# Degree sums by quarters of tokens and a block transpose on VectorE, with pairwise prices for TensorE's changes of use in the planner

## The chip, the cores and the metric

The kernel runs on one core of one Trainium2 chip. The metric is the device time of one execution in microseconds. A core has five engines that work side by side: TensorE (PE, matmuls and transposes; its weight loads are shown as PEld), VectorE (DVE), ScalarE (ACT), GpSimd (POOL) and SyncE (SP, which here only issues transfers). Each works through its own list of instructions in order and waits on semaphores for the others.

## What is computed

There are 64 independent graphs of 256 nodes with 256 features each, in float32, with an adjacency matrix of 256x256 for each. Four layers follow one another, and each is wrapped in `x = layernorm(x + layer(x))`. The change concerns the first layer:

```python
X = heads(lrelu(node_feats @ W_lin + b_lin))      # 4 heads of 64 features
q = heads(lrelu(node_feats @ W_q))
k = heads(lrelu(node_feats @ W_k))
att = sigmoid(einsum('bhxd,bhyd->bhxy', q, k) * scale)
adj_h = adj[:, None] * att
deg = sum(adj_h, axis=-1)                         # one number per head and node
dis = where(deg > 0, deg ** -0.5, 0)
A = dis[..., :, None] * adj_h * dis[..., None, :]
Y = einsum('bhxy,bhyd->bhxd', A, X)               # then a layernorm
```

Layer 1 is a masked softmax attention with 8 heads of 32 features, layer 2 a neighbour sum with an MLP of width 1024, layer 3 a graph attention with one head.

## The kernel before

**Layout.** A node index of 256 is two blocks of 128 partitions (`NB = 2`), and a tile of kind "s" holds 2 x 256 columns. For layer 0 the products `adj_h` are kept transposed: the partition is the node that is summed over, the columns are (head, block, node). `att` is that tile, 128 x 2048.

**The degrees (lines 441 to 465).** L445 adds the two blocks of summed nodes on DVE into two tiles `added`, each for two heads, with columns (head, node). L450 sums over the 128 partitions on PE: its weights are a 128x32 tile of ones, so that each head's sums for 256 nodes land, 32 times over, on a group of 32 partitions of `ps`. The four heads use the four groups of 32 columns of PE's array. Now the nodes lie along the columns, and they are wanted along the partitions. L453 copies the sums to SBUF on ACT (`deg`), L458 transposes the two 128x128 blocks on PE into another PSUM buffer (`pd`), and `D8` picks one of every 32 columns, which gives 8 numbers for each partition: for each block of nodes, four heads. L462 clamps them on DVE, L463 raises them to the power -0.5 on POOL, L464 puts 0 where the degree is 0 (`dis`), L468 scales the values `v` with it. L476 is the matmul with `att`, and after it `dis` scales the result.

**The planner.** The program is written as operations with an engine, an estimated cost in ns, the tiles read and written, and for PE a mode: "full", "rows" (the array split into groups of rows, L433 and L515), "columns" (split into groups of columns, L450, L476 and L551) or "transpose". `Plan.order` simulates the five engines with these costs and puts the operations of all graphs, which lie at different layers at the same time, in one order. Of all operations that are ready it always takes the one that can start first; among equals the one that is due first. An operation that needs a tile waits for a free buffer of its kind in this simulation; PSUM ("p") has 8. The resulting order is each engine's list of instructions. What counts here for PE is one line: an operation of another mode than the last one can start later by `CHANGE[mode]`, where `mode` is the one that is left.

```python
CHANGE = {"full": 0, "rows": 100, "columns": 140, "transpose": 60}
start = max(clock[op.engine] + (CHANGE[mode] if op.engine == "PE" and op.mode != mode else 0), op.ready)
```

So before, the same number served to choose and to advance PE's clock in the simulation. `SLOTS` gives the buffers of each kind, `PE_MM` the cost of a matmul over 256 columns (432 ns) and `PE_TR` that of a transpose (109 ns).

Of the kernel before, what the change touches and what calls it, by code (L numbers as in the profile page):

```python
# [11 lines left out]
OP = mybir.AluOpType  # L12

P = 128
NEG = -9000000000000000.0
TINY = 1.1754944e-38
# [3 lines left out]
PE_MM, PE_TR = 432, 109  # L20
AFTER = {"PE": 230, "DVE": 150, "ACT": 190, "POOL": 180, "SP": 3000}
ITSELF = {"PE": 0, "DVE": 95, "ACT": 110, "POOL": 60, "SP": 0}
CHANGE = {"full": 0, "rows": 100, "columns": 140, "transpose": 60}
TABLE_LOAD = 1430

DMA_KB, DMA_SEEN = 4, 1900

WORDS = {"s": 516, "d": 1024, "b": 2048, "c": 32, "p": 512, "h": 1024}
AHEAD = 12
NEAR = 1, 1, 3  # L30

ROUND = 0, 2, 5, 7
# [43 lines left out]
class Plan:  # L76
# [9 lines left out]
    def op(self, engine, cost, fn, w=(), r=(), turn=None, mode="full", after=None, size=0):  # L86
        pair = lambda x: x if isinstance(x, tuple) else (x, None)
        w, r = [pair(x) for x in w], [pair(x) for x in r]
        op = Op(engine, cost, fn, w, r, self.graph, turn, mode, after, size)
        op.table = turn is not None and engine == "ACT"  # L90
        if op.table:
            self.turns[turn] = self.turns.get(turn, 0) + 1
        self.ops.append(op)

    def order(self):
        for i, op in enumerate(self.ops):
            op.index = i
        for op in reversed(self.ops):
            op.due = min((nxt.due for nxt in op.after), default=4 * (min(op.graph + ROUND[3], self.graphs - 1 + TAIL[3]) + 1))
            if op.turn is not None:  # L100
                op.due = min(op.due, op.turn)
        clock = {e: 0.0 for e in AFTER}
        self.free = {k: [(0.0, i) for i in range(n)] for k, n in SLOTS.items()}
        turns, left = sorted(self.turns), dict(self.turns)
        turn, loaded, mode, moved = 0, None, "full", 0.0
        ready = {op for op in self.ops if not op.waits}
        done = []
        self.busy = {e: 0.0 for e in AFTER}
        while ready:
            best = None  # L110
            for op in ready:
                if (op.due - AHEAD if op.first else op.turn or 0) > turns[turn]:
                    continue
                start = max(clock[op.engine] + (CHANGE[mode] if op.engine == "PE" and op.mode != mode else 0), op.ready)
                need = {}
                for v in op.values:
                    if v.slot is None:
                        need[v.kind] = need.get(v.kind, 0) + 1
                for kind, n in need.items():
                    free = self.free[kind]  # L120
                    if len(free) < n:
                        break
                    start = max(start, sorted(free)[n - 1][0])
                else:
                    key = start, op.due, op.graph, op.index
                    if best is None or key < best[0]:
                        best = key, start, op
            if best is None:
                raise RuntimeError(f"the plan is stuck at {len(done)} of {len(self.ops)}")
            _, start, op = best  # L130
            op.start = start
            ready.discard(op)
            if op.table and op.turn != loaded:
                op.start, loaded = op.start + TABLE_LOAD, op.turn
            if op.engine == "PE":
                mode = op.mode
            end = clock[op.engine] = op.start + op.cost
            op.landed = end + op.seen
            if op.engine == "SP":
                moved = max(moved, end) + op.size * DMA_KB  # L140
                op.landed = max(op.landed, moved + DMA_SEEN)
            self.busy[op.engine] += op.cost
            done.append(op)
            op.takes = [v for v in op.values if v.slot is None]
            for v in op.takes:
                self.free[v.kind].sort()
                v.slot = self.free[v.kind].pop(0)[1]
            for v in op.values:
                v.uses -= 1
                v.end = max(v.end, op.landed)  # L150
                if not v.uses:
                    self.free[v.kind].append((v.end, v.slot))
            for nxt in op.after:
                nxt.waits -= 1
                nxt.ready = max(nxt.ready, end + ITSELF[op.engine] if nxt.engine == op.engine != "SP" else op.landed)
                if not nxt.waits:
                    ready.add(nxt)
            if op.table:
                left[op.turn] -= 1
                while turn < len(turns) - 1 and not left[turns[turn]]:  # L160
                    turn += 1
        assert len(done) == len(self.ops)
        self.span = max(op.start + op.cost for op in done)
        return sorted(done, key=lambda op: op.start)


def two(v):

    return v.t.rearrange("p (n c) -> p n c", n=2)
# [69 lines left out]
def graph(plan, nc, c, t, out, b):  # L239

    op = plan.op
    pe, dve, act, pool = nc and nc.tensor, nc and nc.vector, nc and nc.scalar, nc and nc.gpsimd
    NB = DB = 2
    N = D = 256
    H0, H1 = 4, 8
# [21 lines left out]
    def transposed(src):  # L267
        ps = Value("p", "ps", 2)
        transpose(lambda: two(ps), lambda: two(src), ps, src)
        return ps  # L270
# [27 lines left out]
    def copy(ps, name):  # L298
        dst = Value("s", name, 2)
        op("ACT", 466, lambda: act.copy(dst.t, ps.t), [dst], [ps])  # L300
        return dst
# [111 lines left out]
    for w, name in ((c.w0_q, "qT0"), (c.w0_k, "kT0")):  # L413
        ps = feature_major(w, xT)
# [4 lines left out]
    ps = token_major(xT, lambda: c.w0_l.t, [c.w0_l])  # L419
# [8 lines left out]
    def fn(pss=pss):  # L428
        for hp in range(H0 // 2):
            for m in range(NB):  # L430
                for i in range(2):
                    s = slice(i * HD0, (i + 1) * HD0)
                    pe.matmul(two(pss[2 * hp + i])[:, m, :], two(kT)[s, hp, m * P:(m + 1) * P], two(qT)[s, hp, :],  # L433
                              start=True, stop=True)
# [6 lines left out]
    ps = Value("p", "ps")  # L441
    added = [Value("s", "added") for _ in range(H0 // 2)]
# [3 lines left out]
           [added[i]], [(att, 2 * i), (att, 2 * i + 1)])  # L446

    def fn(ps=ps):
        for h in range(H0):
            pe.matmul(ps.t[h * 32:(h + 1) * 32, :N], c.ones, two(added[h // 2])[:, h % 2], start=True, stop=True)  # L450
    op("PE", PE_MM, fn, [ps], added, mode="columns")
    deg = Value("s", "deg")
    op("ACT", 258, lambda ps=ps: act.copy(deg.t[:, :N], ps.t[:, :N]), [deg], [ps])  # L453
    pd = Value("p", "ps")

    def fn():
        for n in range(NB):
            pe.transpose(pd.t[:, n * P:(n + 1) * P], deg.t[:, n * P:(n + 1) * P], c.ident)  # L458
    op("PE", 2 * PE_TR, fn, [pd], [deg], mode="transpose")
    dp, dis = Value("c", "dp"), Value("c", "dis")  # L460
    D8 = lambda: pd.t[:, :N].rearrange("p (g k) -> p g k", k=32)[:, :, 0]
    op("DVE", 50, lambda: dve.tensor_scalar(dp.t[:, :8], D8(), TINY, None, op0=OP.max), [dp], [pd])  # L462
    op("POOL", 1610, lambda: pool.tensor_tensor(dp.t[:, :8], dp.t[:, :8], c.mhalf, OP.pow), [dp], [dp])  # L463
    op("DVE", 83, lambda: dve.scalar_tensor_tensor(dis.t[:, :8], D8(), 0.0, dp.t[:, :8], op0=OP.is_gt, op1=OP.mult),  # L464
       [dis], [pd, dp])
    by_head = lambda ap: ap.rearrange("p (g d) -> p g d", d=HD0)
    dis_b = lambda: dis.t[:, :8, None].to_broadcast([P, NB * H0, HD0])
# [1 line left out]
    ps = Value("p", "ps", 2)  # L469
# [9 lines left out]
    y = Value("s", "y", 2)  # L479
    if b < NEAR[0]:  # L480
        ps = transposed(copy(ps, "yT"))
# [9 lines left out]
    mv, m = stats(y)  # L491
# [7 lines left out]
    ps = feature_major(c.w1_q, xT)  # L499
# [8 lines left out]
    for hq in range(H1 // 4):  # L508
# [9 lines left out]
        for pair in range(2):  # L518
            e = Value("d", "e", 4)
            for i in range(2):  # L520
                softmax(pss[2 * pair + i], negmask, HD1 ** -0.5, e,
                        lambda n, i=i, e=e: e.t[:, 256 * (2 * i + n):256 * (2 * i + n + 1)],
                        lambda n, i=i: 2 * i + n, r, lambda n, h=4 * hq + 2 * pair + i: 2 * h + n, turn(1, EXP))
            if b < NEAR[1]:
                eT = Value("d", "eT", 2)
                for i in range(2):
                    half = lambda v, i=i: v.t[:, 512 * i:512 * (i + 1)].rearrange("p (n c) -> p n c", n=2)
                    ps = Value("p", "ps", 2)
# [28 lines left out]
    ps = Value("p", "ps")  # L557
# [20 lines left out]
    ps = Value("p", "ps", 2)  # L578
# [10 lines left out]
    for j in range(0, HB, 2):  # L589
        ps = Value("p", "ps", 2)  # L590
# [17 lines left out]
    ps = Value("p", "ps")  # L608
# [21 lines left out]
    ps = Value("p", "ps", 2)  # L630
# [11 lines left out]

    xT3 = copy(transposed(x), "xT3") if b >= plan.graphs - NEAR[2] else far_transposed(x, "xT3")
    v3 = Value("s", "v3", 2)
    V3 = lambda: v3.full.rearrange("p (n c) -> p n c", n=2)
    s1 = lambda n: V3()[:, n, D:D + 1]
    for n in range(NB):
        ps = Value("p", "ps")
# [23 lines left out]
    ps = token_major(eT, lambda: V3()[:, :, :D], [v3])  # L672
    y3 = Value("s", "y", 2)
    mv, m = stats(ps, r3)
# [8 lines left out]
def gnn_stack_kernel(ctx: ExitStack, tc: tile.TileContext, t: dict, out: bass.AP):  # L683
# [36 lines left out]
    for b in range(B):  # L720
        plan.graph = b
        graph(plan, nc, c, t, out, b)
# [43 lines left out]
```

## Time and profile before

| | before |
|---|---|
| time, median of 3 runs | 2791.36 us (2789.9 to 2795.58) |
| span of the profiled execution | 2787.5 us |
| PE busy | 2739.8 us, 98% |
| DVE busy | 2483.4 us, 89% |
| ACT busy | 2138.6 us, 77% |
| POOL busy | 582.3 us, 21% |
| sums L450 on PE | 512 instructions, 40.2 us busy |
| copy L453 on ACT | 64 instructions, 23.9 us busy |
| transposes L458 on PE | 128 instructions, 24.7 us busy |

A row of the groups reads: line, engine, operation, output and inputs by their names in the program, output and input shapes, number of instructions; then busy time in us, mean duration in ns; then the idle time of the engine before these instructions and which instruction ended most of it. In a row of the timeline the first number is the start in us, the second how long the group of instructions lasted. Durations of matmuls overlap, so that for PE the starts tell more than the durations. In the view of waits a row gives who waited for whom, the sum in us, the number of waits and the longest.

### The profile page before, as it was taken

To read this page: it belongs to the slowest core of one execution; us is meant where nothing else is said; L and a number is where in the kernel's file an instruction comes from. 1 tells how busy PE (TensorE), PEld (TensorE's weight loads), DVE (VectorE), ACT (ScalarE), POOL (GpSimd) and SP (SyncE) were. 2 spreads that over 40 slices of the span, in tenths; PEclk is the share of its full clock that TensorE was granted. 3 is DMA by queue.
4 is the path that set the end of the run, shared out by engine and by line. 5 is a ranking of instruction groups with operands and counts; after the bars stand their busy time and mean duration, and the time that the engine had idled before them with its cause. 6 is when DMAs were issued, how large, how long until landed. Compare 5 with 4: busy or idle time off the path is not lost.

```text
span 2787.5 us, 54969 instructions
## 1 busy us (share of the span) xinstructions
PE 2739.8 (98%) x17140; PEld 2191.9 (79%) x17140; DVE 2483.4 (89%) x7748; ACT 2138.6 (77%) x5064; POOL 582.3 (21%) x902
## 2 busy tenths in 40 slices
PE   8999999999999999999999999999999999999997
PEld 6777788787787877877787777787778877788776
DVE  5889999899988999899989988898989899899976
ACT  4778778788778787877777777778878777778775
POOL 1112222122121121221221221212212122122112
PEclk9999999999999999999999999999999999999999
DMA  5676756465663766565656655475665566566540
GB/s 152 193 198 177 209 161 198 148 183 159 200 168 107 219 188 184 155 177 170 192 152 183 196 164 147 139 206 152 197 174 167 155 191 182 159 195 183 158 133 20
DMA packets 546947, 473.08 MB, mean 170 GB/s; under 512 B 177376, under 2 KB 505952, under 8 KB 546656
## 3 DMA queue, kind: packets, MB, share of 16 engines
q1 hardware_dynamic: 546656, 469.58, 58.4%
q8 instruction: 137, 2.24, 0.4%
q14 instruction: 154, 1.26, 0.2%
HBM read 287.45 MB, written 181.93 MB: 168 GB/s over the span
## 4 chain that ended last, share of the span: by engine, by line
PE 87%; DVE 7%; ACT 3%; DMA 1%; issue 1%; POOL 1%; SPq 0%; DVEq 0%; POOLq 0%; ACTq 0%
PE ps L309 15%; PE ps L637 15%; PE ps L320 15%; PE ps L594 14%; PE ps L515 5%; PE ps L433 4%; PE ps L476 4%; PE ps L582 4%; PE av L551 4%; PE ps L652 3%; PE ps L264 2%; ACT e L401 1%; PE ps L450 1%; DVE eb L536 1%; DVE st L334 1%
## 5 line engine op out<-in xcount | busy, mean ns | idle before, releaser
L401 ACT ACTIVATE e<-e,low 128x256 f32<-128x256 f32 x1152 | 576.1, 502 | 74.6 <-DVE low L396 73.3
L637 PE MATMUL ps<-w,hT 128*128 128x256 f32 x2048 | 479.8, 382 | 5.5 <-ACT hT L628 5.5
L594 PE MATMUL ps<-aggT,w 128*128 128x256 f32 x2048 | 471.6, 382 | 2.8 <-DVE y L377 1.6
L346 POOL TENSOR_SCALAR mv<-mv 128x2 f32<-128x2 f32 x384 | 126.9, 331 | 1627.7 <-DVE mv L336 1108.8
L594 PEld LDWEIGHTS ps<-aggT,w 128*128 128x128 f32 x2048 | 381.5, 190 | 72.6 <-issue 8.3
L637 PEld LDWEIGHTS ps<-w,hT 128*128 128x128 f32 x2048 | 381.4, 190 | 67.5 <-issue 10.8
L396 DVE CUSTOM_DVE_ANT_0 e<-ps,adj 128x256 f32<-128x256 f32 x1024 | 361.5, 420 | 33.6 <-PE ps L515 27.0
L347 POOL TENSOR_TENSOR mv<-mv,mhalf 128x2 f32<-128x2 f32 x384 | 304.2, 792 | 32.0
L536 DVE STREAM_TRANSPOSE eb<-e 128x1024 f32<-128x1024 f32 x252 | 306.0, 1225 | 4.3 <-ACT e L401 4.2
L599 ACT ACTIVATE hT<-ps,b 128x256 f32<-128x256 f32 x512 | 229.0, 473 | 89.1 <-PE ps L594 61.7
L361 ACT ACTIVATE x<-y,mv 128x256 f32<-128x256 f32 x384 | 215.7, 597 | 67.3 <-DVE mv L357 59.9
L334 DVE BATCH_NORM_STATS2 st<-y 128x6 f32<-128x256 f32 x640 | 243.4, 412 | 1.2
L401 ACT ACTIVATION_READ_ACCUMULATOR e<-e,low 128x1 f32 x1152 | 220.8, 192 | 0.0
L624 DVE SCALAR_TENSOR_TENSOR hT<-hT,r,pr 128x256 f32<-128x256 f32 x512 | 206.0, 473 | 9.0 <-PE pr L621 9.0
L605 DVE TENSOR_TENSOR sq<-sq 128x512 f32<-128x512 f32 x192 | 130.8, 681 | 67.8 <-ACT sq L602 66.5
L439 DVE TENSOR_TENSOR att<-att,adjT 128x512 f32<-128x512 f32 x256 | 166.2, 676 | 2.5 <-ACT att L437 2.5
L602 ACT ACTIVATE sq<-hT 128x512 f32<-128x512 f32 x256 | 162.3, 634 | 1.2
L515 PE MATMUL ps<-kT,qT 32*128 32x256 f32 x2048 | 148.1, 398 | 0.0
L463 POOL TENSOR_TENSOR dp<-dp,mhalf 128x8 f32<-128x8 f32 x64 | 108.3, 1692 | 185.7 <-DVE dp L462 137.9
L628 ACT ACTIVATE hT<-hT 128x1024 f32<-128x1024 f32 x128 | 130.7, 1052 | 18.7 <-DVE hT L624 14.0
L437 ACT ACTIVATE att<-ps 128x512 f32<-128x512 f32 x256 | 132.2, 602 | 11.1 <-PE ps L637 5.6
L309 PE MATMUL ps<-x0T,w_q 128*128 128x256 f32 x512 | 128.9, 387 | 5.9 <-DMA x0T<-in_xT 5.9
(113 smaller groups left out, 5523.5 us busy)
## 6 DMA issues: line engine op xcount, KB each, us to landing
far<-eb SPq DMA_DIRECT2D x252, 512.0 KB, 3.4
eT<-far SPq DMA_DIRECT2D x1008, 128.0 KB, 3.7
adj<-in_adj SPq DMA_DIRECT2D x128, 256.0 KB, 4.8
x0T<-in_xT SPq DMA_DIRECT2D x64, 256.0 KB, 3.6
adjT<-in_adjT SPq DMA_DIRECT2D x64, 256.0 KB, 4.6
x<-in_x SPq DMA_DIRECT2D x64, 256.0 KB, 4.9
adj<-in_adjT SPq DMA_DIRECT2D x64, 256.0 KB, 3.4
rb<-far SPq DMA_DIRECT2D x512, 32.0 KB, 1.9
```

The lines of the kernel that those rows point to most:

```text
L309: pe.matmul(two(ps)[:, o, :], w.t[:, k, o * P:(o + 1) * P], two(xT)[:, k, :], start=(k == 0), stop=(k == DB - 1))
L320: pe.matmul(two(ps)[:, n, :], two(xT)[:, k, n * P:(n + 1) * P], w()[:, k, :], start=(k == 0), stop=(k == DB - 1))
L334: op("DVE", 328, lambda n=n: dve.bn_stats(st.t[:, 6 * n:6 * n + 6], two(src)[:, n, :]), [(st, n)], [(src, n)])
L347: pool.tensor_tensor(m()[:, :, 2], m()[:, :, 2], c.mhalf[:, :NB], OP.pow)
L361: op("ACT", 492, lambda n=n: act.activation(two(dst)[:, n, :], two(src)[:, n, :], AF.Identity, bias=m()[:, n, 0:1], scale=m()[:, n, 2:3]), ...
L396: op("DVE", 345, lambda n=n: dve.tensor_tensor_reduce(out=E(n), in0=two(logits)[:, n, :], in1=two(negmask)[:, n, :], scale=-scale, scalar= ...
L401: op("ACT", 491, lambda n=n: act.activation(E(n), E(n), AF.Exp, bias=low.t[:, n:n + 1], scale=-1.0, accum_out=r.t[:, col(n):col(n) + 1]), ...
L515: pe.matmul(two(pss[i])[:, n, :], two(qT1)[s, hq, n * P:(n + 1) * P], two(kT1)[s, hq, :], start=True, stop=True)
L536: op("DVE", 1155, lambda e=e, eb=eb: dve.transpose(eb.t.rearrange("p (b g i) -> p g b i", b=4, i=32), e.t.rearrange("p (g b i) -> p g b i" ...
L594: pe.matmul(two(ps)[:, i, :], c.w2_1.t[:, k, (j + i) * P:(j + i + 1) * P], two(aggT)[:, k, :], start=(k == 0), stop=(k == DB - 1))
L599: op("ACT", 357, lambda ps=ps, i=i, j=j: act.activation(Hb(j + i)[:, 0], two(ps)[:, i, :], AF.Identity, bias=c.b2_1.t[:, j + i:j + i + 1]) ...
L637: pe.matmul(two(ps)[:, n, :], Hb(j)[:, 0, n * P:(n + 1) * P], c.w2_2.t[:, j, :], start=(j == 0), stop=(j == HB - 1))
```

## The change

It has two parts. In the first, the sums of the degrees are laid out so that no transpose on PE is needed. Each of the four groups of 32 columns of PE's array now takes a quarter of the nodes of every block of 128 instead of a head: for each of the two `added` tiles and each group, one matmul over 4 x 32 = 128 columns. On the partitions of group g, then, stand the sums of nodes 32 g to 32 g + 31 of each block, along the columns and the same in all 32 rows. A transpose of each 32x32 block, which DVE does in one instruction for the whole 128x256 tile, brings each node's sum to its partition, in SBUF. The copy on ACT, the transposes on PE and the second PSUM buffer fall away. The eight numbers of a partition come in the order (head, block) and are read as (block, head), so what follows is as before.

In the second part the planner prices PE's changes of use by pairs of modes, and it separates two things: the choice of the next operation uses one plain number, `STAY` (100, less 60 if the operation is a transpose), for leaving rows or columns; PE's clock in the simulation then moves by the price of the pair. Two operations of the same tiled mode have a price too. Leaving a transpose is free.

```diff
-CHANGE = {"full": 0, "rows": 100, "columns": 140, "transpose": 60}
+CHANGE = {("full", "rows"): 92, ("full", "columns"): 92, ("rows", "full"): 315, ("columns", "full"): 240,
+          ("rows", "columns"): 212, ("columns", "rows"): 136, ("rows", "rows"): 103, ("columns", "columns"): 70, ("transpose", "rows"): 92,
+          ("transpose", "columns"): 92, ("rows", "transpose"): 260, ("columns", "transpose"): 192}
...
+STAY = 100
...
-                start = max(clock[op.engine] + (CHANGE[mode] if op.engine == "PE" and op.mode != mode else 0), op.ready)
+                start = clock[op.engine]
+                if op.engine == "PE" and mode in ("rows", "columns") and mode != op.mode:
+                    start += STAY - 60 * (op.mode == "transpose")
+                start = max(start, op.ready)
...
             if op.engine == "PE":
+                op.start = max(op.start, clock["PE"] + CHANGE.get((mode, op.mode), 0))
                 mode = op.mode
...
     def fn(ps=ps):
-        for h in range(H0):
-            pe.matmul(ps.t[h * 32:(h + 1) * 32, :N], c.ones, two(added[h // 2])[:, h % 2], start=True, stop=True)
+        for i in range(2):
+            for g in range(4):
+                pe.matmul(ps.t[g * 32:(g + 1) * 32, i * P:(i + 1) * P], c.ones,
+                          added[i].t.rearrange("p (m g t) -> p m g t", g=4, t=32)[:, :, g], start=True, stop=True)
     op("PE", PE_MM, fn, [ps], added, mode="columns")
-    deg = Value("s", "deg")
-    op("ACT", 258, lambda ps=ps: act.copy(deg.t[:, :N], ps.t[:, :N]), [deg], [ps])
-    pd = Value("p", "ps")
-
-    def fn():
-        for n in range(NB):
-            pe.transpose(pd.t[:, n * P:(n + 1) * P], deg.t[:, n * P:(n + 1) * P], c.ident)
-    op("PE", 2 * PE_TR, fn, [pd], [deg], mode="transpose")
+    pd = Value("s", "deg")
+    op("DVE", 340, lambda ps=ps: dve.transpose(pd.t[:, :N], ps.t[:, :N]), [pd], [ps])
     dp, dis = Value("c", "dp"), Value("c", "dis")
-    D8 = lambda: pd.t[:, :N].rearrange("p (g k) -> p g k", k=32)[:, :, 0]
+    D8 = lambda: pd.t[:, :N].rearrange("p (h n k) -> p n h k", n=NB, k=32)[:, :, :, 0]
```

In the two DVE operations that use `D8` only the view of `dp` and `dis` as (block, head) is new.

More of the change, by code (lines that the diff above doesn't have):

```diff
@@ L448, in fn @@
     def fn(ps=ps):
-        for h in range(H0):
-            pe.matmul(ps.t[h * 32:(h + 1) * 32, :N], c.ones, two(added[h // 2])[:, h % 2], start=True, stop=True)
+        for i in range(2):
+            for g in range(4):
+                pe.matmul(ps.t[g * 32:(g + 1) * 32, i * P:(i + 1) * P], c.ones,
+                          added[i].t.rearrange("p (m g t) -> p m g t", g=4, t=32)[:, :, g], start=True, stop=True)
     op("PE", PE_MM, fn, [ps], added, mode="columns")
-    deg = Value("s", "deg")
-    op("ACT", 258, lambda ps=ps: act.copy(deg.t[:, :N], ps.t[:, :N]), [deg], [ps])
-    pd = Value("p", "ps")
-    def fn():
-        for n in range(NB):
-            pe.transpose(pd.t[:, n * P:(n + 1) * P], deg.t[:, n * P:(n + 1) * P], c.ident)
-    op("PE", 2 * PE_TR, fn, [pd], [deg], mode="transpose")
+    pd = Value("s", "deg")
+    op("DVE", 340, lambda ps=ps: dve.transpose(pd.t[:, :N], ps.t[:, :N]), [pd], [ps])
     dp, dis = Value("c", "dp"), Value("c", "dis")
-    D8 = lambda: pd.t[:, :N].rearrange("p (g k) -> p g k", k=32)[:, :, 0]
-    op("DVE", 50, lambda: dve.tensor_scalar(dp.t[:, :8], D8(), TINY, None, op0=OP.max), [dp], [pd])
+    D8 = lambda: pd.t[:, :N].rearrange("p (h n k) -> p n h k", n=NB, k=32)[:, :, :, 0]
+    op("DVE", 50, lambda: dve.tensor_scalar(dp.t[:, :8].rearrange("p (n h) -> p n h", n=NB), D8(), TINY, None, op0=OP.max), [dp], [pd])
     op("POOL", 1610, lambda: pool.tensor_tensor(dp.t[:, :8], dp.t[:, :8], c.mhalf, OP.pow), [dp], [dp])
-    op("DVE", 83, lambda: dve.scalar_tensor_tensor(dis.t[:, :8], D8(), 0.0, dp.t[:, :8], op0=OP.is_gt, op1=OP.mult),
+    op("DVE", 83, lambda: dve.scalar_tensor_tensor(
+        dis.t[:, :8].rearrange("p (n h) -> p n h", n=NB), D8(), 0.0, dp.t[:, :8].rearrange("p (n h) -> p n h", n=NB), op0=OP.is_gt, op1=OP.mult),
        [dis], [pd, dp])
```

## The prediction

> **What bounds the kernel now.** I read the first part of the page, then the waits of TensorE (PE), then its groups by shape, then the timeline of PE in places where its use changes. The busy shares first:
>
> ```profile
> PE 2739.8 (98%) x17140; PEld 2191.9 (79%) x17140; DVE 2483.4 (89%) x7748; ACT 2138.6 (77%) x5064; POOL 582.3 (21%) x902
> PE 87%; DVE 7%; ACT 3%; DMA 1%; issue 1%; POOL 1%; SPq 0%; DVEq 0%; POOLq 0%; ACTq 0%
> ```
>
> PE is busy nearly all the time, and the chain that ended last is 87% PE. Next, whom PE waits for:
>
> ```profile
> PE ps L309 <- DMA x0T<-in_xT: 5.9, 1, 5.9
> PE ps L637 <- ACT hT L628: 5.5, 2, 3.0
> PE ps L320 <- DVE yT L568: 2.8, 2, 2.3
> PE ps L320 <- ACT eT L300: 2.6, 4, 1.0
> PE ps L264 <- ACT e L401: 2.0, 4, 0.6
> ```
>
> All waits of this view add to about 33 us, and 5.9 of that is the start. So what PE has to do sets the time, and what leaves PE is gained nearly whole. But busy isn't work: the ends of matmuls are modelled. So I read starts, where PE passes from one kind of use to another:
>
> ```profile
> 1011.89 1.89 PE L320 MATMUL ps<-v,eT 128*128 128x256 f32 x8
> 1013.71 1.95 PE L476 MATMUL ps<-att,v 128*64 128x256 f32 x16
> 1015.59 0.64 PE L450 MATMUL ps<-added,ones 128*32 128x256 f32 x8
> 1016.16 1.13 PE L320 MATMUL ps<-w_v,xT 128*128 128x256 f32 x4
> 1017.13 0.50 PE L612 MATMUL ps<-mean_of,sq 128*128 128x1 f32 x4
> ...
> 1020.40 0.43 PE L621 MATMUL pr<-ident,rs 128*128 128x128 f32 x2
> 1020.66 0.38 PE L458 MATMUL ps<-ident,deg 128*128 128x128 f32 x2
> 1020.88 0.27 PE L558 MATMUL ps<-ident,r 128*16 128x128 f32 x1
> 1020.99 1.03 PE L309 MATMUL ps<-x0T,w_q 128*128 128x256 f32 x4
> 1021.86 0.59 PE L309 MATMUL ps<-x0T,w_k 128*128 128x256 f32 x2
> ```
>
> Each float32 matmul of the program is two instructions here, so a matmul over 256 columns is two passes of 216 ns (L309 takes 1021.86 - 1020.99 = 0.87 us for four). A transpose is one instruction of 109 ns: the two of L458 take 1020.88 - 1020.66 = 0.22 us, and L558 to L309 is 0.11, so going from a transpose to a full matmul costs nothing. Tiled uses do cost: eight full passes before L476 take 1.82 instead of 8 x 0.216 = 1.73, so 0.09 on entry; L450, eight instructions in four column groups, takes 1016.16 - 1015.59 = 0.57 instead of 2 x 0.216 = 0.43, and the four passes after it 0.97 instead of 0.86, so 0.14 + 0.11 on exit. For rows:
>
> ```profile
> 1029.74 2.00 PE L433 MATMUL ps<-qT,kT 64*128 64x256 f32 x16
> 1031.66 3.72 PE L637 MATMUL ps<-w,hT 128*128 128x256 f32 x16
> 1035.22 0.38 PE L661 MATMUL ps<-ident,v 128*128 128x128 f32 x2
> ```
>
> L433 takes 1.92 instead of 8 x 0.216 = 1.73, and the sixteen after it 3.56 instead of 3.46: 0.19 + 0.10 on exit. An excursion to columns thus costs about 0.09 + 0.25 = 0.34 us, one to rows about 0.09 + 0.29 = 0.38. Counted over the whole timeline PE leaves rows 175 times and columns 113 times, so 175 x 0.38 + 113 x 0.34 = 105 us go into changes. The planner before charges 100 and 140 ns on leaving and nothing on entry: 175 x 0.10 + 113 x 0.14 = 33 us.
>
> **What the Trainium skill says.** "TensorEngine Tiling (Array Packing)", Key Properties: changing the tiling mode drains TensorE. The trace agrees (0.09 to 0.19 us at each border), and shows no drain between transposes and full matmuls. "TensorE: Matmul & The Clock Gate", section LDWEIGHTS, prices a weight load at columns / 1.2 ns: 107 ns for 128 columns, which is the 0.10 seen behind an exit, and 27 ns for the 32 columns of L450. "VectorE: DVE Perf Modes", The three transpose paths: the DVE transpose works in 32x32 blocks only and writes SBUF. That is why the sums are laid out by quarters of tokens; its 311 ns is for bf16, so I take its time from the trace below.
>
> **The change, part by part.** There are 64 graphs. These rows carry the prices:
>
> ```profile
> L450 PE MATMUL ps<-added,ones 128*32 128x256 f32 x512 | 40.2, 386 | 0.0
> L551 PE MATMUL av<-eT,v 128*32 128x256 f32 x2048 | 123.9, 382 | 0.4 <-DVE low L396 0.4
> L458 PE MATMUL ps<-ident,deg 128*128 128x128 f32 x128 | 24.7, 275 | 0.0
> ```
> ```profile
> L276 DVE STREAM_TRANSPOSE eb<-ps 128x512 f32<-128x512 f32 x63 | 44.2, 702 | 9.3 <-PE ps L476 8.7
> L536 DVE STREAM_TRANSPOSE eb<-e 128x1024 f32<-128x1024 f32 x252 | 306.0, 1225 | 4.3 <-ACT e L401 4.2
> ```
>
> 1. Removed from PE: the two transposes of a graph, 2 x 109 ns x 64 = 14.0 us. From first starts to the next group's, L458 takes 19.2 us in all over the timeline; the 5.2 above 14.0 are waits and weight loads beside a tiled use. Those waits may only move, so I count 2 of them. Gain 16.
>
> 2. The sums: eight matmuls over 128 columns instead of four over 256, so 16 instructions instead of 8 in four column groups: four rounds of four at about 109 ns = 436, where there were two of 216 = 432. A weight load of 27 ns lies behind a pass of 109. The data now come in runs of 32 elements; L551 reads eT in runs of 32 too, and its 32 instructions take 8 x 0.22 us (1020.40 - 1018.53 = 1.87 with entry and exit), so runs cost nothing. If the load were not hidden, it is 4 x 27 ns x 64 = 7 us; that is the upper end. I take 0.5 us.
>
> 3. ACT loses the copy at L453, 64 x 0.374 = 24 us of an engine at 77%. It isn't on PE's path except by delays; I count 0.
>
> 4. DVE gains a block transpose of 128x256 out of PSUM. From 702 ns for 512 and 1225 for 1024, a column costs (1225 - 702) / 512 = 1.02 ns, so 256 cost 702 - 261 = 441 ns; the cheapest 128x256 operation beside it (0.40 us at L365) is the lower end. 64 x 0.44 = 28 us, DVE goes from 2483 to about 2511 us, 90%. PE's own work hides it as long as DVE keeps 270 us idle. Behind it on DVE stand the softmax reductions of L396, whose output ACT waits for, and through ACT the transposes and matmuls of PE. The wait for PE that ACT had at L453 (54.7 us in 31 cases, all of ACT's idle time) becomes one of DVE: the queue is in order, so a sum that PE does late stops the rest of DVE. ACT was stopped that way and PE hardly noticed; I count +2 us, up to 10.
>
> 5. PSUM: the transposed degrees held one of the 8 buffers from L458 to the end of L464, across the power on POOL (1.69 us): median 8.4 us in the timeline, 64 x 8.4 = 540 us of buffer time. They lie in SBUF now. The read at L462 and L464 stays 8 elements for each partition (0.15 us). Relief for a planner that waits for free buffers; I count 2 us of gain.
>
> 6. The planner. Its new prices agree with the trace: 92 for an entry (0.09), 240 from columns to full (0.25), 315 from rows to full (0.29), and leaving a transpose is free now. Its choice gets a plain 100 for leaving a tiled use, 40 if it goes to a transpose; before it was 100 for rows, 140 for columns, 60 for transposes. So the choice changes little, but PE's clock in the plan, which ran about 105 - 33 = 72 us ahead of the chip, becomes right: at a choice more operations are ready, those with the nearest due times go first, and fewer waits of 0.3 to 5 us are left in the stream. About 27 us of waits stand after the start, and changes of 105 us. I take a fifth of the waits, 5 us, and 1 us for exits by way of a transpose (0.31 to 0.16 behind them is 0.05 less than to a full matmul). Gain 6. No row bounds this well: a new order of 17140 instructions can shift the time by 10 us either way.
>
> Sum: -16 + 0.5 + 2 - 2 - 6 = -21.5, from 2791.4 to about 2770.
>
> **The rivals.** (a) Only the transposes count: the plan is as good as the old one, and the waits at L458 reappear elsewhere: 2791.4 - 14.0 = 2777; with the weight loads of the narrow passes exposed (7 us), 2784. For it: the choice has nearly the same weights. Against: a clock wrong by 72 us. (b) The plan is much better: a tenth of the 288 excursions merged (29 x 0.36 = 10 us) and half of the 27 us of waits gone (14): 2770 + 6 - 24 = 2752. For it: nothing merges them now beyond a small penalty. Against: the penalty did not grow. (c) Slower: DVE becomes what PE waits for. If the 28 us of transposes arrive whole in PE's waits, 2791.4 - 14.0 + 28 = 2805; a worse order, with 10% more excursions (10 us) and waits of 10 more, gives 2797. For it: DVE is at 89% and has little room in some slices; leaving columns is 40 ns cheaper in the choice than before. Against: no wait of PE for DVE is above 2.8 us in total now.
>
> **How the numbers follow.** I give 0.55 to the forecast (2760 to 2776 around 2770), 0.22 to (a), 0.13 to (b) and 0.10 to (c). The limit of 0.2% is 5.6 us, so faster ends at 2785.8 and slower begins at 2797. The forecast, (b) and nearly all of (a) are faster: 0.83. Of (a) and the mild part of (c) 0.09 fall within; 0.08 for slower. The range goes from 2750, just below (b), to 2789, past the worst of (a) with a small loss to DVE.
>
> **What would show each step.** Right: no transposes of deg on PE; PE busy about 20 us less while its share stays at 98%; the sums' 16 instructions at 128 columns in starts of four about 109 ns apart, 0.5 to 0.6 us for a graph up to the next group; a DVE block transpose of 128x256 at 0.40 to 0.45 us; ACT without the copy. For step 6: waits of PE below 28 us in total and about 280 exits from tiled uses. Wrong: starts of 216 ns for the narrow passes (then 28 us are lost and the gain is gone), PE waits for DVE of 10 us or more, or over 310 exits from tiled uses.

## The result and the profile after

| | before | after |
|---|---|---|
| time, median | 2791.32 us | 2778.74 us (2776.96 to 2782.11) |
| ratio after / before | | 0.9955 (0.9942 to 0.9967) |
| span of the profiled execution | 2787.5 us | 2776.9 us |
| PE busy | 2739.8 us | 2721.9 us |
| DVE busy | 2483.4 us | 2495.9 us |

The change saves 12.6 us, 0.45%. The forecast was 21.5 us. From here on line numbers are those of the kernel after, where L450 has become L458, L476 L480, L551 L555, L515 L519, L309 L316, L320 L327 and L594 L598; lines of the runs below are each kernel's own. First the busy shares and the chain that ended last:

```profile
PE 2721.9 (98%) x17524; PEld 2187.8 (79%) x17524; DVE 2495.9 (90%) x7812; ACT 2119.0 (76%) x5000; POOL 577.7 (21%) x902
PE 72%; DVE 16%; ACT 5%; DMA 3%; issue 2%; SPq 2%; POOL 1%; DVEq 0%; POOLq 0%; ACTq 0%
```

PE is still 98% busy, with 18 us less. But the chain holds 72% PE where it held 87%, and DVE 16% where it held 7%: PE now waits for others along the way more often. The sums and the block transpose, in the views of PE's and DVE's groups and of single lines (durations as least, median and most, in ns):

```profile
L458 PE MATMUL ps<-added,ones 128*32 128x128 f32 x1024 | 41.1, 278 | 0.0
```
```profile
L462 DVE STREAM_TRANSPOSE deg<-ps x64: 407/432/449, 26.0 to 2597.7; 128x256 f32<-128x256 f32 x64
...
its engine sat idle before it (us, times) until:
who waited for it (us, times):
  PEld ps L519: 0.3, 1
```

The sixteen narrow passes are as busy as the eight wide ones were (41.1 against 40.2 us). The block transpose takes 432 ns, 441 were worked out. Nothing stands under its idle time: this view shows no wait of DVE for the sums of PE. And a place in the timeline of PE:

```profile
1019.27 1.95 PE L480 MATMUL ps<-att,v 128*64 128x256 f32 x16
1021.15 1.93 PE L555 MATMUL av<-eT,v 128*32 128x256 f32 x32
1022.90 0.62 PE L458 MATMUL ps<-added,ones 128*32 128x128 f32 x16
1023.45 2.01 PE L519 MATMUL ps<-kT,qT 32*128 32x256 f32 x32
1025.45 0.61 PE L616 MATMUL ps<-mean_of,sq 128*128 128x1 f32 x4
```

Four tiled uses follow each other here, and the sums take 1023.45 - 1022.90 = 0.55 us, with no entry to pay behind L555, which is split in the same way. The first waits of PE:

```profile
PE ps L316 <- DMA x0T<-in_xT: 11.1, 2, 5.9
PE ps L327 <- ACT eT L307: 4.7, 5, 1.5
PE ps L616 <- ACT v L660: 4.3, 10, 0.4
PE ps L641 <- ACT hT L632: 3.4, 2, 3.2
PE ps L598 <- DVE low L403: 3.2, 10, 0.5
PE ps L616 <- DVE sq L611: 2.1, 11, 0.2
```

All waits of this view add to about 39 us; before it was 30 (the prediction had 33). Of the first row 5.9 us are the start, and 5.2 are one wait for the input of a later graph, 111 us into the run, that the order of before doesn't have. The view leaves out the short waits. So I also went through the starts of all matmuls and counted as a wait what a distance has above the usual one: 216 ns in a row of full passes, 109 of transposes, 309 at a border of a tiled use, 104 more behind an exit. Before, waits so counted are 64 us of the 2765 from the first start to the last; after, 78 of 2755. The level depends on which distances are called usual; the differences between kernels matter here. Without waits PE's time fell from 2701 to 2677, by 23.5 us; 13.5 of it came back as waits. Of the 23.5, the transposes are 14. The rest goes with fewer changes of use: PE leaves rows 173 and columns 100 times (175 and 113 before), and of these exits 112 go to a transpose (36 before).

### The profile page after: what moved, and what is told of

The parts are those of the page before. It is cut to its first block, busy times and chain, and to the rows that moved or that the text cites. A ratio compares the mean times of both kernels' runs of the same rounds, so it can differ in the third digit from the quotient of the medians.

```text
span 2776.9 us, 55677 instructions
## 1 busy us (share of the span) xinstructions
PE 2721.9 (98%) x17524; PEld 2187.8 (79%) x17524; DVE 2495.9 (90%) x7812; ACT 2119.0 (76%) x5000; POOL 577.7 (21%) x902
## 4 chain that ended last, share of the span: by engine, by line
PE 72%; DVE 16%; ACT 5%; DMA 3%; issue 2%; SPq 2%; POOL 1%; DVEq 0%; POOLq 0%; ACTq 0%
PE ps L598 13%; PE ps L316 12%; PE ps L327 11%; PE ps L641 11%; PE ps L480 4%; PE av L555 3%; PE ps L440 3%; PE ps L519 3%; PE ps L586 3%; PE ps L656 3%; DVE st L341 2%; ACT e L408 2%; DVE eb L540 2%; PE ps L271 2%; DVE hT L628 2%
## 5 line engine op out<-in xcount | busy, mean ns | idle before, releaser
L408 ACT ACTIVATE e<-e,low 128x256 f32<-128x256 f32 x1152 | 576.6, 503 | 61.5 <-DVE low L403 60.4
L598 PE MATMUL ps<-aggT,w 128*128 128x256 f32 x2048 | 472.4, 381 | 4.1 <-DVE low L403 3.2
L598 PEld LDWEIGHTS ps<-aggT,w 128*128 128x128 f32 x2048 | 380.5, 190 | 66.2 <-DVE low L403 15.8
L519 PE MATMUL ps<-kT,qT 32*128 32x256 f32 x2048 | 145.6, 397 | 1.6 <-DVE low L403 0.9
L316 PE MATMUL ps<-x0T,w_q 128*128 128x256 f32 x512 | 132.1, 393 | 11.1 <-DMA x0T<-in_xT 11.1
```

The lines of the kernel that those rows point to most:

```text
L316: pe.matmul(two(ps)[:, o, :], w.t[:, k, o * P:(o + 1) * P], two(xT)[:, k, :], start=(k == 0), stop=(k == DB - 1))
L408: op("ACT", 491, lambda n=n: act.activation(E(n), E(n), AF.Exp, bias=low.t[:, n:n + 1], scale=-1.0, accum_out=r.t[:, col(n):col(n) + 1]), ...
L519: pe.matmul(two(pss[i])[:, n, :], two(qT1)[s, hq, n * P:(n + 1) * P], two(kT1)[s, hq, :], start=True, stop=True)
L598: pe.matmul(two(ps)[:, i, :], c.w2_1.t[:, k, (j + i) * P:(j + i + 1) * P], two(aggT)[:, k, :], start=(k == 0), stop=(k == DB - 1))
```

## The experiments

Two questions stood: where did half of the gain go, and which part of the change brought what is left? The trouble with such a kernel is that every edit of an operation lets the planner make a new order. So the first runs keep an order and change the work in it. Differences in us are of medians: those against before use its runs in the same session (2791.3, 2791.3 and 2791.0), those against after its 2778.7 of the first measurement. The intervals are of the ratio to before.

**The order of before, the new layout.** The plan is given the old operations; only what they emit is new (the sums as in the kernel after; the cut shows the two operations behind them). So the orders of all other instructions are those of before. The plan still counts a copy on ACT and knows nothing of DVE's block transpose.

```diff
-    op("ACT", 258, lambda ps=ps: act.copy(deg.t[:, :N], ps.t[:, :N]), [deg], [ps])
+    op("ACT", 258, lambda ps=ps: dve.transpose(deg.t[:, :N], ps.t[:, :N]), [deg], [ps])
...
-    op("PE", 2 * PE_TR, fn, [pd], [deg], mode="transpose")
+    op("PE", 2 * PE_TR, lambda: None, [pd], [deg], mode="transpose")
```

> The new layout of the sums put into the order of before: the old planner plans the old operations, and the block transpose stands where the copy stood, nothing where the two transposes of PE stood. Theory A (PE's work sets the time, each transpose is worth its 109 ns): 64 x 2 x 109 ns = 14 us less than before, 2775 to 2779. Theory B (the 28 us that DVE gains come back as waits of PE): half of that or less, 2784 to 2791. Theory C (the gain of the change is the planner's): no difference, 2790 to 2793.

It took 2791.66 us, ratio 1.0002 (0.9994 to 1.0011): nothing is gained. The transposes are gone, and PE's busy time fell by 6 us only:

```profile
PE 2733.9 (98%) x17524; PEld 2195.3 (79%) x17524; DVE 2500.6 (90%) x7812; ACT 2120.0 (76%) x5000; POOL 582.1 (21%) x902
```

PE's waits, counted over the starts, rose from 64 to 78 us, as much as was removed. The time speaks against A; it lies in the range of C and just past that of B. Two runs ask what became of the 14 us.

**The same without DVE's block transpose.** The copy stays on ACT, and the degrees are read from it untransposed, so the kernel leaves the transposition out. The cut is against the run above.

```diff
-    op("ACT", 258, lambda ps=ps: dve.transpose(deg.t[:, :N], ps.t[:, :N]), [deg], [ps])
+    op("ACT", 258, lambda ps=ps: act.copy(deg.t[:, :N], ps.t[:, :N]), [deg], [ps])
```

> As layout_old_order (the order of before, the sums by quarters, no transposes of PE), but the copy of ACT stays and DVE does no block transpose: the transposition itself is left out. Theory B1 (in this order the work that DVE gains, and its wait for the sums in its own queue, take back what PE lost): 14 us less than before, 2775 to 2780. Theory B2 (in this order PE's 14 us aren't on the path at all: what follows the transposes waits for something else): no difference, 2788 to 2793.

2780.65 us, ratio 0.9967 (0.9954 to 0.9979): 10.6 us less than before, at the edge of what B1 gave (2775 to 2780) and far from B2. So taking the transposes off PE is worth 10.6 of their 14 us in this order, and giving DVE the block transpose in place of ACT's copy costs 11 us (2791.66 - 2780.65). The layout's gain is real, and its own cost on DVE cancels it in this order.

**The kernel before with as much work added to DVE**, and nothing that waits for it (`spare` is a tile that nobody reads):

```diff
-    op("ACT", 258, lambda ps=ps: act.copy(deg.t[:, :N], ps.t[:, :N]), [deg], [ps])
+    def fn(ps=ps):
+        act.copy(deg.t[:, :N], ps.t[:, :N])
+        dve.transpose(c.spare, c.w0_q.t[:, 0, :])
+    op("ACT", 258, fn, [deg], [ps])
```

> The kernel before in its own order, with a block transpose of 128x256 from a weight to a spare tile added to DVE at the place of each copy of ACT: 28 us of DVE and no new wait for PE or ACT. Theory B1, if the load is what costs: about 14 us more than before, 2801 to 2809. If only the wait for the sums costs: 2790 to 2795. Theory B2: 2790 to 2795.

```profile
L455 DVE STREAM_TRANSPOSE spare<-w_q x64: 401/435/443, 26.5 to 2608.3; 128x256 f32<-128x256 f32 x64
its engine sat idle before it (us, times) until:
who waited for it (us, times):
```

Nobody waits for these instructions and DVE doesn't wait before them, yet the time is 2797.94 us, ratio 1.0024 (1.0015 to 1.0033): 6.7 us for 64 x 0.435 = 28 us of DVE. That lies between the two ranges expected, half of the 14 us expected if the load is what costs, but clear of no difference. So DVE's load by itself delays PE, by what comes behind it in DVE's list; what makes up the other 4.3 of the 11 us wasn't taken apart.

**The order of after, with two idle transposes more on PE for each graph, and with the block transpose done twice:**

```diff
             pe.transpose(pr.t[:, n * P:(n + 1) * P], rs.t[:, n:n + 1].to_broadcast([P, P]), c.ident)
+        for n in range(NB):
+            pe.transpose(pr.t[:, N + n * P:N + (n + 1) * P], c.ident, c.ident)
```

> The kernel after, in its own order, with two transposes of the constant identity added to PE for each graph, behind those of L625 and into an unused half of their buffer; nobody waits for them and the plan doesn't know them. Theory A: 14 us more than after, 2791 to 2795. If PE had room for them (its waits would shrink by as much), 0 to 7 us more, 2779 to 2786.

```diff
-    op("DVE", 340, lambda ps=ps: dve.transpose(pd.t[:, :N], ps.t[:, :N]), [pd], [ps])
+    def fn(ps=ps):
+        for _ in range(2):
+            dve.transpose(pd.t[:, :N], ps.t[:, :N])
+    op("DVE", 340, fn, [pd], [ps])
```

> The kernel after in its own order, the block transpose done twice: 28 us more on DVE. If DVE's work is on the path as PE's is (two_more cost 13 us for 14): 2790 to 2805. If PE alone bounds it: 2777 to 2783.

Two transposes more: 2792.02 us, 13.3 more than after, for 14.0 us of work. PE has no room in this order. The block transpose twice: 2796.42 us, 17.7 more than after, for 28 us of DVE. So both engines are on the path at once: in this order a microsecond more of PE costs 0.95, one of DVE 0.63 (in that of before 0.76 and 0.24). In the waits of PE for the doubled kernel (whose L601 is the line that was L598 above) more waits for DVE stand at the MLP's first matmul, 7.5 us where after had 3.2:

```profile
PE ps L601 <- DVE low L403: 7.5, 11, 1.0
```

**One part of the change alone.** `layout_only` is the kernel before with the new sums and block transpose, planned anew by the old planner; `planner_only` is the kernel after with the old sums, copy and transposes.

> The new layout with the old planner, which makes a new order for it. The plan leaves rows 182 times and columns 122 times, 16 more than before, worth 16 x 0.36 = 6 us. Theory A: 2791 - 14 + 6 = 2783, 2778 to 2788, so an order can eat half of what the layout brings. Theory B: 2786 to 2797. Theory C: 2790 to 2793.

> The new planner with the old layout. The plan leaves rows 163 times and columns 108 times, 17 fewer than before, worth 17 x 0.36 = 6 us. Theory A: 2791 - 6 and some waits more or less, 2780 to 2792. Theory C: all 12 us of the change, 2777 to 2781.

The layout alone: 2785.87 us, ratio 0.9976 (0.9967 to 0.9986), 5.4 us less than before; this is in the range of theory A, which charged 6 us for 16 exits more. In this kernel the plan knows of DVE's block transpose. From here the new planner brings the other 7.1 us (2785.87 - 2778.74). The planner alone: 2816.09 us, ratio 1.0081 (1.0068 to 1.0095), 24.8 us more, though it has 17 exits fewer. That was outside of every expectation, and C, by which the planner alone brings the gain, falls with it. Two parts of -5 and +25 us together make -13, so they don't add: the new planner is worth 7.1 us with the new layout and costs 24.8 with the old one. In `planner_only` PE waits for engines that hardly stopped it before:

```profile
PE ps L316 <- DMA x0T<-in_xT: 12.1, 2, 6.3
PE ps L327 <- ACT eT L307: 11.6, 21, 2.4
PE pr L628 <- POOL rs L623: 10.0, 18, 0.6
PE ps L601 <- DVE low L403: 4.0, 4, 2.6
```

Before, these waits for ACT's `eT` were 2.6 us and those for POOL's `rs` 0.4.

**The planner's two halves, each with the new layout.** `old_clock` has the new choice and moves PE's clock by the old prices; `old_choice` has the new clock and chooses by the old prices. `LEAVE` holds the old prices (0, 100, 140 and 60).

```diff
-                op.start = max(op.start, clock["PE"] + CHANGE.get((mode, op.mode), 0))
+                op.start = max(op.start, clock["PE"] + (LEAVE[mode] if op.mode != mode else 0))
```

> The kernel after with the new choice (100 and 40 for leaving), but PE's clock in the plan moved by the old prices (100, 140, 60 on leaving, nothing on entry). The plan leaves rows 185 and columns 127 times, 39 more than after's 173 and 100. If the right clock is what the planner brings: 39 x 0.36 = 14 us more than after, 2788 to 2798. If the order is a matter of chance: anything from 2770 to 2815. If the new choice is what helps: 2776 to 2782.

```diff
-                start = clock[op.engine]
-                if op.engine == "PE" and mode in ("rows", "columns") and mode != op.mode:
-                    start += STAY - 60 * (op.mode == "transpose")
-                start = max(start, op.ready)
+                start = max(clock[op.engine] + (LEAVE[mode] if op.engine == "PE" and op.mode != mode else 0), op.ready)
```

> The kernel after with the new clock (prices by pairs) but the old choice (100, 140 and 60 for leaving rows, columns and transposes). The plan leaves rows 178 and columns 107 times, 12 more than after's. If the right clock is what helps (old_clock without it gained nothing): 2776 to 2785. If it takes both: 2788 to 2795. If orders are chance: up to 2815.

`old_clock`: 2791.42 us, ratio 1.0000 (0.9992 to 1.0009). `old_choice`: 2812.80 us, ratio 1.0078 (1.0065 to 1.0090). So the new choice without the right clock gains nothing, and the right clock with the old choice gives an order 21.8 us slower than before.

**The one number of the choice.** The kernel after with `STAY` at 120 and 60 instead of 100, and the old layout with the new planner and 120:

```diff
-STAY = 100
+STAY = 120
```

> The kernel after with STAY = 120 instead of 100: nothing but the order differs, the plan leaves rows 175 and columns 102 times, 4 more than after's. If time follows from PE's work, changes and DVE's load: 2778 to 2782. If orders that a small number calls up differ by themselves: off by more than 5 us either way.

> The kernel after with STAY = 60, so that transposes are entered free and the rest costs 60 in the choice. The plan leaves rows 183 and columns 123 times, 33 more than after's, with the right clock. If the changes of use set the time: 33 x 0.36 = 12 us more than after, 2787 to 2795. If the right clock does, whatever the number of changes: 2776 to 2783.

> The old layout with the new planner and STAY = 120 instead of 100: rows are left 175 and columns 106 times. planner_only took 25 us more than before. If the new planner does harm to the old layout as such: 2806 to 2822. If that one order was bad by chance: 2780 to 2800.

2784.77 us, ratio 0.9976 (0.9965 to 0.9986); 2803.20 us, 1.0047 (1.0035 to 1.0060); 2824.46 us, 1.0117 (1.0102 to 1.0133). With 120 only the order differs from after, by four exits, and 6 us are lost, more than a theory of work and exits allowed; 60 and the old layout with 120 came out above each of their expected ranges. The old layout was slow in both orders of the new planner; two orders aren't enough to say that it always is.

All orders side by side. Exits are the times that PE leaves rows or columns, waits are PE's as counted over the starts of one profiled execution (that of planner_only took 2824.7 us, the slowest of its five):

| kernel | layout | order by | us | exits | PE's waits, us |
|---|---|---|---|---|---|
| before | old | old planner | 2791.3 | 288 | 64 |
| planner_only | old | new planner | 2816.1 | 271 | 111 |
| po_stay120 | old | new, STAY 120 | 2824.5 | 281 | 112 |
| layout_old_order | new | order of before | 2791.7 | 288 | 78 |
| layout_only | new | old planner | 2785.9 | 304 | 75 |
| old_clock | new | new choice, old clock | 2791.4 | 312 | 80 |
| old_choice | new | old choice, new clock | 2812.8 | 285 | 102 |
| stay60 | new | new, STAY 60 | 2803.2 | 306 | 96 |
| stay120 | new | new, STAY 120 | 2784.8 | 277 | 81 |
| after | new | new | 2778.7 | 273 | 78 |

The number of exits doesn't sort the times: 285 exits stand at 2812.8 and 304 at 2785.9. The waits nearly do: every order above 2800 us has 96 us or more. That says where the time is and not why, since time less waits differs by only about 13 us among the orders of the new layout. In `old_choice`, the slowest order of the new layout, waits are long at three places that lie one behind the other, ACT for DVE, DVE for PE, and PE for ACT and DVE, as the views of the three engines show:

```profile
ACT e L405 <- DVE low L400: 110.1, 75, 5.5
```
```profile
DVE y L381 <- PE ps L638: 61.8, 17, 6.0
```
```profile
PE ps L324 <- ACT eT L304: 8.6, 13, 2.4
PE ps L595 <- DVE y L381: 7.1, 9, 0.8
```

In the kernel after the same three are 60.4 us (ACT for `low`), 11.2 (DVE for the second matmul of the MLP) and 4.7 (PE for `eT`). That the three drive each other in a ring is a guess from these sums; in `planner_only`, as slow, the first two are only 25.7 and 17.1 us, and before, 73.3 and 36.4. What makes an order fall into such waits, and whether it could be seen in the plan, stays open.

## Why the prediction was right, and where its sizes were off

The time fell, and it lies in the range. That PE's work is on the path held. That PE hides nearly all of DVE's new work did not hold. The sum of the steps was 8.9 us too large. Taken in the sequence of the steps, the layout planned by the old planner brought 5.4 us, where steps 1 to 5 make 15.5; the new planner then brought 7.1, where step 6 made 6. So what is missing is missing in the layout.

That the total came out in the range is in part luck. With the same layout and the same right clock, `STAY` 60 and the old choice take 2803.2 and 2812.8 us, past the upper end of 2789. And the number is nearer to rival (a), 2777, than to the forecast, though not for the reason of (a): with the order of before the layout gained nothing.

1. The transposes, -16: removed alone in a fixed order they are worth 10.6 us, and added to after 13.3. The 14.0 us of work were right and are worth most of their size in both orders; no run shows the 2 us of waits on top of them.

2. The sums, +0.5: right. Four rounds start 109 to 110 ns apart, the first 133. From the first start to the next group's the sums took 569 ns in the median before and, in the same order, 574 with the new layout (`layout_old_order`). Neither the runs of 32 elements nor the weight loads cost anything. The prediction took 27 ns for such a load; the trace shows 110, but loads overlap (before, at 1015.59 us, eight of them lie within 0.16 us):

```profile
L458 PEld LDWEIGHTS ps<-added,ones x1024: 106/110/173, 25.3 to 2590.4; 128*32 128x32 f32 x171
```

3. ACT, 0: its copy left (64 instructions, 24 us less work), and no run takes away the copy alone.

4. DVE, +2 and at most 10: this is the term that was mis-sized. The duration was right (432 ns for 441), but in the order of before the step costs 11 us, in that of after doubling it costs 17.7, and mere load without any wait 6.7. In none of these three did the plan know of the added work; with a plan that does, its cost can't be read by itself. The reason given was wrong too: the fear was that DVE would stand still before the sums, and it hardly does (no wait in after, 0.9 us in `layout_old_order`). I had read "no wait of PE for DVE is above 2.8 us" as room on DVE. But from before to `layout_old_order` PE's listed waits for DVE rose only from 9.9 to 14.2 us in all, over several lines, while the step cost 11; in after they are 9.0, none above 3.2, so the sign set for this term, 10 us or more, stayed silent. That every buffer which DVE fills or frees comes later, and PE waits in many places for less than that view shows, fits these numbers but wasn't followed wait by wait.

5. PSUM, -2: not tried by itself.

6. The planner, -6, "by 10 us either way": the size fits by chance, the spread was far too small. With the new layout the new planner is worth 7.1 us against a new plan of the old one, and 12.9 (2791.66 - 2778.74) against the order of before, which wasn't made for this layout; with the old layout it costs 24.8. The cause given, a clock that is right, isn't shown: with the right clock stand orders of 2778.7, 2784.8, 2803.2 and 2812.8 us. Nor was the clock as far off as 72 us: the sum left out the 60 ns that the old plan charged for leaving a transpose, 260 times in the trace or 16 us, so about 56 were left. Of the two signs, about 280 exits came true (273), and waits of PE below 28 us didn't (39 in the view). The new planner found a good order for the new layout with its number at 100; a general gain from its better prices isn't shown by any run.

So the change's 12.6 us can be split in two ways, and each is right only along its own path: -5.4 from the layout under the old planner and -7.1 from the new one; or, with the order of before held, -10.6 from PE, +11.0 from DVE and -12.9 from an order made anew. Of the rivals, (c) named the right force: DVE took back all that PE gave in the order of before, though not twice as much. None of the other kernels run beats the one after.

## What to carry to other kernels

Where two engines are at 90% and more in one planned order, work that is moved from one to the other has to be charged on both sides; here the exchange was worth nothing in a fixed order, and 5.4 us with a new plan of the same planner. To price a move, keep the order and take each half of it alone, and load the receiving engine with work that nobody waits for: the small waits in the profile of before don't tell how much it can bear. A change to a planner is judged by several orders, not by one, since a spread of 34 us among seven orders of the same work is larger than what the change was for.

## What was unexpected in the hardware

A tiled group of four weight loads and passes keeps its full rate at half the width: in the same order sixteen passes over 128 columns took 574 ns against 569 for eight over 256. A border behind the sums costs 93 to 94 ns, whatever the width of their passes: from the last pass of the sums to the next use it is 203 ns where the passes are of 109 ns, and 309 before, where they are of 216. What comes behind an exit differs more: a full pass follows another after 320 ns, 104 more than the usual 216, a transpose another after about 160, 51 more than the usual 109. Both load weights of 128 columns, so an exposed load, by which the prediction read the 0.10 us, doesn't give both numbers; the cause stays open.
